# A graph transformer layer on one core: tiles of 125 columns, the values' projection behind the sums, and a different opening

## The chip, the core and the metric

The kernel runs on one core of one Trainium2 chip. The metric is device time in microseconds (us) of one execution, as the median of several runs. A profile is one execution recorded by the hardware. Its engines are TensorE (PE, with its weight loads as PEld), VectorE (DVE), ScalarE (ACT), GpSimd (POOL) and SyncE (SP, which here only issues transfers).

## The reference

The layer takes 3125 nodes of 256 features, 53125 weighted edges sorted by their destination, and the weights of three blocks. All arrays are float32.

```
xn  = layernorm(x)
gnn = segment_sum(edge_weight[:, None] * xn[src], dst) @ W.T + b
q, k, v = xn @ Wq, xn @ Wk, xn @ Wv                # 8 heads of 32
Q, K = elu(q) + 1, elu(k) + 1
KV  = sum over nodes of K^T v, for each head       # 32 x 32 for each of the 8 heads
Z   = 1 / (Q . sum over nodes of K + 1e-6)
msg = layernorm((Q @ KV * Z) @ Wm) * g1 + b1
mix = xn + layernorm(relu([xn, msg] @ W1) @ W2) * g2 + b2
x   = x + gnn + mix
x   = x + ffn(layernorm(x))                        # 16 experts, each node takes the best two
```

What bears on the change is the sum over nodes: `KV = K^T (xn Wv)` is the same as `(K^T xn) Wv`, and the blocks of the heads can be cut out at the end.

## The kernel before

**Tiles.** The 3125 nodes lie in 25 tiles (`NT`) of `V` = 125 nodes. Before the change a tile takes 128 (`P`) rows or columns in most places, of which the last three are padding. Floating point matrices are float32; a float32 matmul is recorded as two MATMUL instructions, a transpose as one.

**The opening.** SP loads the first five tiles of `x` in two transfers (`LOADS`), ACT's queue loads `dst_0` and three weights side by side into `wcat` (L167). PE multiplies ones to keep busy (`busy`, L239), then counts heads of edge lists (L243). DVE takes the mean and variance of the tiles (`stats`, L103 and L104) and their inverse deviations by a chain of thirteen small instructions (`rsqrt`, L91 to L98), one chain for each entry of `BATCHES`: two tiles, three, seven, thirteen. `AHEAD` says at which tile the moments of later tiles are taken. The loads of tiles 5 to 14 wait for the moments of the first batch.

**The projection.** A loop over the tiles runs three things, shifted against each other. In PE's order they stand as T(t+1), P(t), S(t-1):

- `normed(t)`: DVE makes `xn` (L416), PE transposes it in two halves (L428, called T below), ACT copies it to `xnT`.
- `projected(t)`: PE makes messages and keys together, 512 columns wide, in one bank (L437), and values, 256 columns wide, in another (L439); the two are called P. ACT takes exp and relu of the keys, and copies the messages to `y` and the values, with a column of ones behind each half, to `v_sb` (L447). DVE joins the keys (L445). SP stores `y` to DRAM.
- `summed(t)`: PE adds keys times values to `pkv` (L461, 129 columns wide, called S).

Between these DVE, POOL and PE prepare the edge lists in pieces (`windows`, handed out at the tiles that `LISTS` names): the first edge of each group of five nodes, 128 edges gathered behind it, and from them `keys` and `wgts`. Their last steps are three groups of transposes on PE (L309), which stand by T(16), and five conversions on POOL (L317 and L319).

From tile 18 on (`HOT`) each tile also issues two adjacencies. In `adjacency` DVE builds one-hot rows (L335) and weighted ones (L340, L350), PE multiplies twelve pairs of them (L355), ACT copies the result and SP stores it. There are 157 of them; most run in the next stage.

**Behind the sums.** `ksum` and `kv_bd` are the sums of keys and the heads' blocks of `pkv` (L526, L528). PE transposes `kv_bd` (L533) and multiplies it by `Wm` (L538) to give `kvw`. The queries of the first group of tiles (`asked`) are made at tiles 22 and 23 (L477), and are divided by their sums here (L489, four RECIPROCALs of L494).

**The mixer, messages and experts.** Seven groups of four or three tiles go through `mixer` (L641 to L682), where the matmuls of W1 and Wq run over 512 or 384 columns of nodes (L662, L477). Adjacencies and messages (L625) are dealt out between its steps. Then come the last messages (L738) with the gates, and the experts (L1001, L1027).

**Order.** The program is written in one order. The framework places each engine's instructions ahead of time, in that order where their operands are expected to be ready, and later ones ahead where not. Each engine then runs its own list in order.

**PSUM.** There are eight banks: two for adjacencies, two called `big`, three called `tok` and one for `pkv`.

Of the kernel before, what the change touches and what calls it, by code (L numbers as in the profile page):

```python
# [17 lines left out]
N = 3125  # L18
# [35 lines left out]
BATCHES = ((0, 2), (2, 5), (5, 12), (12, 25))  # L54

LISTS = {1: 1, 6: 1, 7: 2, 8: 2, 14: 1, 15: 1, 16: 1}
AHEAD = {1: (2, 5), 2: (5, 9), 3: (9, 12), 4: (12, 15), 6: (15, 17), 9: (17, 21), 10: (21, 25)}
# [5 lines left out]
def tile_gps_layer(ctx: ExitStack, tc: tile.TileContext, a: dict, out: bass.AP):  # L63
# [7 lines left out]
    y_d = dram.tile([NT * P, C], F32, name="y_d")  # L71
# [12 lines left out]
    def rsqrt(var, n, with_last=False):  # L84

        v = small.tile([P, 13], F32, name="rs_v")[:, :n]
        hv = small.tile([P, 13], F32, name="rs_h")[:, :n]
        bits = small.tile([P, 13], I32, name="rs_b")[:, :n]
        y = small.tile([P, 13], F32, name="rs_y")[:, :n]
        s = small.tile([P, 13], F32, name="rs_s")[:, :n]  # L90
# [10 lines left out]
    def stats(mv, src):  # L101
        st = small.tile([P, 6], F32, name="bn_st")
        nc.vector.bn_stats(st, src)  # L103
        return nc.vector.bn_aggr(mv, st)  # L104
# [58 lines left out]
    wcat = w_mix.tile([128, 2, 3 * C], F32, name="wcat")  # L163
    load_x(nc.sync, *LOADS[0])
    nc.scalar.dma_start(dst_0, a["dst"].rearrange("(p j) -> p j", p=V)[:, 0:1])
    for i, name in enumerate(("gnn_WT", "Wk", "Wv")):
        nc.scalar.dma_start(wcat[:, :, i * C : (i + 1) * C], a[name].rearrange("(k p) o -> p k o", p=128))  # L167
    load_x(nc.sync, *LOADS[1])
    wq = w_mix.tile([128, 2, C], F32, name="wq")
    wm = w_mix.tile([128, 2, C], F32, name="wm")  # L170
    w1 = w_mix.tile([128, 4, F], F32, name="w1")
    w2 = w_mix.tile([128, 4, C], F32, name="w2")

    def load_later(t):
# [3 lines left out]
        if t in (11, 13, 15, 17):  # L178
            w, name = ((wm, "Wm"), (wq, "Wq"), (w1, "W1"), (w2, "W2"))[(t - 11) // 2]
            nc.sync.dma_start(w, a[name].rearrange("(k p) o -> p k o", p=128))  # L180
# [16 lines left out]
    xnT = w_mix.tile([128, 2, NT * P], F32, name="xnT")  # L197
# [11 lines left out]
    kv_bd = w_mix.tile([128, 2, 128], F32, name="kv_bd")  # L209
# [9 lines left out]
    def bank_a(of=4 * P):  # L219
        return adj_ps.tile([128, 512], F32, name="pa")[:, :of].rearrange("p (i e) -> p i e", e=of // 4)  # L220

# [7 lines left out]
    def windows():  # L229
# [11 lines left out]
        busy(16)  # L241
# [86 lines left out]
    def adjacency(part, ai, t, n, to):  # L328

        one = hot.tile([128, 2, 2, P, 2], BF16, name="one", bufs=4)  # L330
        wone = hot.tile([128, 2, 3, P, 2], BF16, name="wone")
        if t + 1 < NT:
# [6 lines left out]
            shape = [128, 2, 3, P, 2]  # L339
            nc.vector.tensor_tensor(wone, one[:, :, 1:2, :, :].to_broadcast(shape),  # L340
                                    w[:, :, :, None, :].to_broadcast(shape), op=ALU.mult)
        else:
            for j in range(min(n, 2)):
# [5 lines left out]
                shape = [128, b, 3, P]  # L349
                nc.vector.tensor_tensor(wone[:, :b, :, :, j], one[:, :b, 1:2, :, j].to_broadcast(shape),  # L350
# [941 lines left out]
```

## Time and profile before

| What | Value |
|---|---|
| median of 3 runs | 1037.57 us (1037.27 to 1039.04) |
| the profiled execution | 1038.03 us, of which the span is 1036.2 us |
| PE, share of the span busy | 97% |
| DVE | 63% |
| ACT, POOL | 25%, 21% |
| mean granted PE clock | 0.995 |
| opening and projection | 0 to 111 us |
| mixer with adjacencies and most messages | 121 to 590 us |
| last messages with gates | 591 to 707 us |
| experts | 707 to 1036 us |

The share of a busy engine is taken over its records. PE's records end where a pipeline's model puts the end, so the pace of PE is read from the starts of its instructions: four records of L437 last 1.88 us by their record, while the next line starts 1.72 us later.

### The profile page before, as it was taken

What the parts mean: (1) busy time and instruction counts of PE and PEld (TensorE: products, weight loads), DVE (VectorE), ACT (ScalarE), POOL (GpSimd) and SP (SyncE); (2) the same over time, 40 slices, a digit from 0 to 9 for tenths busy, and PEclk for the clock granted to TensorE, in tenths of its full rate; (3) what the DMA queues carried; (4) which work ended last, traced back from release to release, by engine and by line L of the source; (5) the groups of instructions that cost most, each with busy time, mean ns of one, the idle gap of its engine ahead of it and who ended that gap; (6) DMA issues with size and microseconds to landing.
All of it is one profiled execution on the core that took longest, in us unless ns stands there. A gap on an engine that the chain in (4) does not pass through costs nothing.

```text
span 1036.2 us, 16279 instructions
## 1 busy us (share of the span) xinstructions
PE 1007.1 (97%) x6006; PEld 809.3 (78%) x6006; DVE 655.3 (63%) x1750; ACT 263.9 (25%) x577; POOL 216.1 (21%) x200
## 2 busy tenths in 40 slices
PE   7999999999999999999999999999999999999995
PEld 5667666686786887887877888887888888888884
DVE  8968699889787897956598148786932222222221
ACT  3666424323323233222141000103111111111110
POOL 3420100023100000000000001014445444545442
PEclk9999999999999999999999999999999999999998
DMA  6444104343344344553354455565757757667662
GB/s 214 95 131 145 53 31 167 128 140 136 122 137 138 133 162 133 175 181 143 140 182 155 159 167 166 183 194 179 209 155 226 240 170 234 199 202 225 206 189 26
DMA packets 70374, 165.09 MB, mean 159 GB/s; under 512 B 11091, under 2 KB 29934, under 8 KB 66314
## 3 DMA queue, kind: packets, MB, share of 16 engines
q1 hardware_dynamic: 53816, 138.10, 38.9%
q0 software_dynamic: 15520, 25.04, 10.7%
q8 instruction: 50, 0.82, 0.3%
q10 hardware_dynamic: 946, 0.79, 0.2%
q14 instruction: 42, 0.34, 0.1%
HBM read 105.85 MB, written 58.00 MB: 158 GB/s over the span
## 4 chain that ended last, share of the span: by engine, by line
PE 71%; DVE 10%; issue 1%; POOL 0%; ACT 0%; POOLq 0%; DVEq 0%; ACTq 0%
PE ph L1001 18%; PE pb L625 13%; PE po L1027 10%; PE po L738 8%; PE pa L355 6%; PE big L662 6%; PE tok L673 3%; DVE wone L340 2%; PE ptr L987 1%; PE pa L625 1%; PE big L477 1%; DVE one L335 1%; PE ph L799 1%; DVE wone L350 1%; PE big L489 1%
## 5 line engine op out<-in xcount | busy, mean ns | idle before, releaser
L1001 PE MATMUL ph<-xTb,wt 128*128 128x256 f32 (+2 forms) x992 | 204.5, 355 | 0.8 <-issue 0.8
L1001 PEld LDWEIGHTS ph<-xTb,wt 128*128 128x128 f32 x992 | 171.5, 190 | 24.9 <-ACT xTb L990 4.5
L625 PE MATMUL pb<-y_early,nbr 128*128 128x256 f32 x736 | 170.7, 382 | 0.4 <-DVE x_all L627 0.4
L340 DVE TENSOR_TENSOR wone<-one,wgts 128x1536 bf16<-128x1536 bf16 x150 | 140.6, 949 | 27.0 <-PE pa L355 26.8
L625 PEld LDWEIGHTS pb<-y_early,nbr 128*128 128x128 f32 x736 | 135.4, 190 | 17.2 <-DVE x_all L627 1.0
L355 PEld LDWEIGHTS <-one 128*128 128x128 bf16 x1875 | 117.3, 97 | 39.1 <-issue 19.1
L358 ACT COPY adj<-pa 128x512 f32<-128x512 f32 (+1 forms) x157 | 91.8, 586 | 194.2 <-PE pa L355 156.4
L355 PE MATMUL pa<-wone,one 128*128 128x128 bf16 x1875 | 130.3, 218 | 2.3 <-DVE wone L340 0.9
L1008 DVE TENSOR_TENSOR hid<-hid,ph 128x512 f32<-128x512 f32 (+2 forms) x62 | 38.3, 618 | 145.7 <-PE ph L1001 135.4
L1027 PE MATMUL po<-wt,hid 128*128 128x256 f32 (+1 forms) x456 | 115.2, 385 | 0.8 <-DVE yb L1030 0.7
L738 PE MATMUL po<-y_late,nbr 128*128 128x256 f32 x450 | 102.3, 381 | 0.5 <-DVE x_all L627 0.5
L335 DVE TENSOR_TENSOR one<-iota,keys 128x1024 bf16<-128x1024 bf16 x150 | 100.8, 692 | 0.7 <-POOL wgts L317 0.7
L1031 POOL DMA_INDIRECT out<-yb,to_l x45 | 70.9, 1576 | 114.4 <-DVE yb L1030 63.4
L1027 PEld LDWEIGHTS po<-wt,hid 128*128 128x128 f32 (+1 forms) x456 | 79.1, 184 | 17.6 <-DVE yb L1030 5.5
L738 PEld LDWEIGHTS po<-y_late,nbr 128*128 128x128 f32 x450 | 83.4, 190 | 11.2 <-DVE x_all L627 0.9
L1007 ACT ACTIVATE hid<-ph 128x512 f32<-128x512 f32 (+2 forms) x62 | 33.6, 542 | 208.4 <-PE ph L1001 204.4
L1030 DVE TENSOR_SCALAR yb<-po,sh 128x256 f32<-128x256 f32 (+1 forms) x57 | 27.5, 482 | 57.3 <-PE po L1027 54.9
L751 POOL IOTA rev<- 125x16 f32 x1 | 0.2, 156 | 296.5 <-PE pb L625 296.5
L700 POOL TENSOR_TENSOR x_all<-x_all,cb 128x256 f32<-128x256 f32 x25 | 25.7, 1050 | 148.2 <-DVE x_all L627 140.5
L627 DVE TENSOR_TENSOR x_all<-x_all,pb 128x512 f32<-128x512 f32 (+1 forms) x37 | 24.3, 655 | 41.8 <-PE pb L625 41.8
L662 PE MATMUL big<-xnT,w 128*128 128x512 f32 (+1 forms) x112 | 49.8, 556 | 0.0
L437 PE MATMUL big<-wcat,xnT 128*128 128x512 f32 x100 | 49.0, 612 | 0.0
(285 smaller groups left out, 1202.5 us busy)
## 6 DMA issues: line engine op xcount, KB each, us to landing
wt<-in_w SPq DMA_DIRECT2D x28, 1536.0 KB
adj_d<-adj SPq DMA_DIRECT2D x156, 256.0 KB
nbr<-adj_d SPq DMA_DIRECT2D x25, 576.0 KB
nbr<-adj_d SPq DMA_DIRECT2D x50, 256.0 KB
nbr<-adj_d SPq DMA_DIRECT2D x25, 512.0 KB
wt<-in_w POOLq DMA_DIRECT2D x3, 1536.0 KB
out<-x_all SPq DMA_DIRECT2D x25, 125.0 KB
x_all<-in_x SPq DMA_DIRECT2D x4, 640.0 KB
```

What stands on the lines that cost most here:

```text
L335: nc.vector.tensor_tensor(one.rearrange("p b h e j -> p (b h) e j"), iota_2[:, None, :, :].to_broadcast(shape), ql.rearrange("p b h j -> p ...
L340: nc.vector.tensor_tensor(wone, one[:, :, 1:2, :, :].to_broadcast(shape), w[:, :, :, None, :].to_broadcast(shape), op=ALU.mult)
L355: nc.tensor.matmul(pa[:, j, :], lhsT=one[:, j // 2, 0, :, j % 2], rhs=wone[:, j // 2, i, :, j % 2], start=(i == 0), stop=(i == 2))
L358: copied = nc.scalar.copy(rows[:, :n, :], pa[:, :n, :])
L437: nc.tensor.matmul(pyk, lhsT=xnT[:, k, cols], rhs=wcat[:, k, : 2 * C], start=(k == 0), stop=(k == 1))
L625: nc.tensor.matmul(pb[:, i, :], lhsT=rows[:, k - t0, :], rhs=y_of(k), start=(k == t0 and i == 0), stop=(k == t1 - 1), skip_group_check=True)
L662: nc.tensor.matmul(ph[:, :w], lhsT=w1[:, k, j * 128 : (j + 1) * 128], rhs=rhs, start=(k == 0), stop=(k == 3))
L738: last = nc.tensor.matmul(pg, lhsT=rows[:, k - t0, :], rhs=y_of(k), start=(k == t0), stop=(k == t1 - 1))
L1001: last = nc.tensor.matmul(p[:, m, :w], lhsT=self.wt[:, i, k * F + at : k * F + at + 128], rhs=self.xT[:, k, :w], start=(k == 0), stop=(k = ...
L1008: self.units = nc.vector.tensor_tensor(hid, hid, pre[1], op=ALU.mult)
L1027: last = nc.tensor.matmul(po[:n_r, r, :], lhsT=self.hid[:, k, r * LANES : r * LANES + n_r], rhs=self.wt[:, 2, k * C : (k + 1) * C], start= ...
L1031: made.append(nc.gpsimd.indirect_dma_start(out=out[:, :], out_offset=bass.IndirectOffsetOnAxis(ap=at, axis=0), in_=yb[:n_r, r, :], in_offs ...
```

## The change

**Columns.** Tiles take 125 rows and columns instead of 128: in `xnT`, the transposes, the projections, `y_d`, the adjacencies' weighted rows `wone` and PE's products with them, the queries, the mixer and the messages. Adjacency rows in SBUF keep 128 columns; three buffers (`adj_ring`) have their last three columns set to zero once, by POOL.

**Values.** `Wv` leaves `wcat` and is loaded at tile 9. The projection has no L439 and ACT no copy of values. `xn` gets a column of ones (a ring of six buffers, set by POOL), and the sums run over `xn`: 257 columns wide, each half of the keys in a bank of its own. Behind the sums ACT scales them, PE turns them in four transposes, ACT copies, PE multiplies by `Wv` (eight records of 128 columns) and DVE cuts out the heads' blocks straight into `kvT`; the two old transposes and one copy go.

**PSUM.** `pkv` takes two banks. `tok` has two; when `pkv` is done, one of its banks serves every third `tok`.

**Opening.** The first batch has five tiles, with one chain. The two weights of `wcat` are loaded on SP's queue, behind the first five tiles of `x`. PE keeps busy with 24 products of ones instead of 16.

```diff
-BATCHES = ((0, 2), (2, 5), (5, 12), (12, 25))
+BATCHES = ((0, 5), (5, 12), (12, 25))
-AHEAD = {1: (2, 5), 2: (5, 9), 3: (9, 12), 4: (12, 15), 6: (15, 17), 9: (17, 21), 10: (21, 25)}
+AHEAD = {2: (5, 9), 3: (9, 12), 4: (12, 15), 6: (15, 17), 9: (17, 21), 10: (21, 25)}
...
-    y_d = dram.tile([NT * P, C], F32, name="y_d")
+    y_d = dram.tile([N, C], F32, name="y_d")
...
-    for i, name in enumerate(("gnn_WT", "Wk", "Wv")):
-        nc.scalar.dma_start(wcat[:, :, i * C : (i + 1) * C], a[name].rearrange("(k p) o -> p k o", p=128))
     load_x(nc.sync, *LOADS[1])
+    for i, name in enumerate(("gnn_WT", "Wk")):
+        nc.sync.dma_start(wcat[:, :, i * C : (i + 1) * C], a[name].rearrange("(k p) o -> p k o", p=128))
...
+    def tok(shape):
+        taken_tok.append(0)
+        if spare_ps and len(taken_tok) % 3 == 0:
+            return spare_ps[0].tile(shape, F32, name="tok_3")
+        return a_ps.tile(shape, F32, name="tok")
...
-        busy(16)
+        busy(24)
...
-        wone = hot.tile([128, 2, 3, P, 2], BF16, name="wone")
+        wone = hot.tile([128, 2, 3, V, 2], BF16, name="wone")
...
-                nc.tensor.matmul(pa[:, j, :], lhsT=one[:, j // 2, 0, :, j % 2], rhs=wone[:, j // 2, i, :, j % 2],
+                nc.tensor.matmul(pa[:, j, :V], lhsT=one[:, j // 2, 0, :, j % 2], rhs=wone[:, j // 2, i, :, j % 2],
                                  start=(i == 0), stop=(i == 2))
...
+    xn_ring = [work.tile([P, C + 1], F32, name=f"xn{i}", bufs=1) for i in range(6)]
+    for xn in xn_ring:
+        nc.gpsimd.memset(xn[:, C:], 1.0)
...
-        pv = a_ps.tile([P, C], F32, name="tok", bufs=3)
...
-        for k in range(2):
-            last = nc.tensor.matmul(pv, lhsT=xnT[:, k, cols], rhs=wcat[:, k, 2 * C :], start=(k == 0), stop=(k == 1))
...
-        v_copy = nc.scalar.activation(v_sb[:, :, :128], pv.rearrange("p (c v) -> p c v", c=2), AF.Copy, scale=1.0 / N)
...
-            nc.tensor.matmul(pkv[:, c, :], lhsT=k_sb[:V, c * 128 : (c + 1) * 128], rhs=v_sb[:V, c, :],
-                             start=(t == 0 and c == 0), stop=(t == NT - 1), skip_group_check=True)
+            nc.tensor.matmul(pkv[:, c, : C + 1], lhsT=k_sb[:V, c * 128 : (c + 1) * 128], rhs=xn[:V, :],
+                             start=(t == 0), stop=(t == NT - 1))
...
-    nc.vector.tensor_tensor(kv_bd, same_head[:, None, :].to_broadcast(shape), pkv[:, :, :128], op=ALU.mult)
+    k_by = work.tile([128, 2, C], F32, name="k_by", bufs=1)
+    nc.scalar.activation(k_by, pkv[:, :, :C], AF.Copy, scale=1.0 / N)
+    turned_k = a_ps.tile([128, 512], F32, name="big")
+    for c in range(2):
+        for k in range(2):
+            nc.tensor.transpose(turned_k[:, (2 * k + c) * 128 : (2 * k + c + 1) * 128],
+                                k_by[:, c, k * 128 : (k + 1) * 128], ident)
+    by_k = work.tile([128, 2, 2, 128], F32, name="by_k", bufs=1)
+    nc.scalar.copy(by_k.rearrange("p k c n -> p (k c n)"), turned_k)
+    pvk = tok([128, 2, 128])
+    for c in range(2):
+        for k in range(2):
+            nc.tensor.matmul(pvk[:, c, :], lhsT=wv[:, k, c * 128 : (c + 1) * 128], rhs=by_k[:, k, c, :],
+                             start=(k == 0), stop=(k == 1))
+    kvT = work.tile([128, 2, 128], F32, name="msgT", bufs=1)
+    nc.vector.tensor_tensor(kvT, same_head[:, None, :].to_broadcast(shape), pvk, op=ALU.mult)
```

## The prediction

> **What bounds the kernel now.** I read the page's busy shares first, then busy time by stretch, then the timeline of PE, DVE and POOL up to 125 us, then the groups by line.
>
> ```profile
> PE 1007.1 (97%) x6006; PEld 809.3 (78%) x6006; DVE 655.3 (63%) x1750; ACT 263.9 (25%) x577; POOL 216.1 (21%) x200
> ...
> 14.00:16.00 2.00, 1.47 (x4) 0.81 (x5) 2.00 (x11) 0.37 (x1) 1.52 (x2) 0.78 0.82 303
> 16.00:18.00 2.00, 2.00 (x4) 0.84 (x3) 2.00 (x10) 0.00 (x0) 1.56 (x2) 0.50 0.45 137
> 26.00:52.00 26.00, 26.00 (x115) 17.52 (x114) 23.70 (x81) 15.97 (x49) 11.29 (x13) 1.00 0.46 95
> ```
>
> PE is busy throughout, and its clock (the number before the last two) is whole except at 14 to 19 us. DVE is close behind: 23.70 of 26 us in the projection.
>
> ```profile
> 9.11 1.99 PE L437 MATMUL big<-wcat,xnT 128*128 128x512 f32 x4
> 14.53 0.41 PE L428 MATMUL tok<-ident,xn 128*128 128x128 f32 x2 [2.57 <-DVE less L391]
> 14.77 3.27 PE L437 MATMUL big<-wcat,xnT 128*128 128x512 f32 x4
> 19.72 1.88 PE L437 MATMUL big<-wcat,xnT 128*128 128x512 f32 x4
> ...
> 35.97 1.88 PE L437 MATMUL big<-wcat,xnT 128*128 128x512 f32 x4
> 37.69 1.03 PE L439 MATMUL tok<-wcat,xnT 128*128 128x256 f32 x4
> 38.55 0.61 PE L461 MATMUL pkv<-v_sb,k_sb 125*128 125x129 f32 x4
> 39.00 0.39 PE L428 MATMUL tok<-ident,xn 128*128 128x128 f32 x2
> 39.22 1.88 PE L437 MATMUL big<-wcat,xnT 128*128 128x512 f32 x4
> ```
>
> The opening: P(0) at 9.11, then PE stands 2.57 us for T(2), whose `xn` waits for the second chain of deviations; P(1) then runs at half clock, and P(2) starts at 19.72. From there a tile takes 3.25 us with no gap: 1.72 for L437, 0.86 for L439, 0.45 for L461, 0.22 for the transposes, start to start.
>
> ```profile
> 54.67 0.73 DVE L416 TENSOR_SCALAR xn<-x_all,mv,rs_y 128x256 f32<-128x256 f32 x2
> 61.75 0.70 PE L309 MATMUL pa<-ident,key 125*128 125x125 f32 x5
> 71.15 0.83 POOL L317 CAST wgts<-turned 128x650 bf16<-128x650 f32 x1
> 74.24 1.72 PE L355 MATMUL pa<-wone,one 128*128 128x128 bf16 x24 [0.43 <-DVE wone L340]
> ...
> 111.10 0.42 DVE L526 TENSOR_TENSOR ksum<-same_head,pkv 128x256 f32<-128x256 f32 x1 [0.94 <-PE pkv L461]
> 113.15 3.37 DVE L494 RECIPROCAL eq<-eq 128x256 f32<-128x256 f32 x2 [1.30 <-ACT eq L493]
> 121.81 3.90 PE L641 MATMUL tok<-kvw,qT 128*128 128x256 f32 x16 [0.95 <-DVEq L559]
> ...
> L340 DVE TENSOR_TENSOR wone<-one,wgts 128x1536 bf16<-128x1536 bf16 x150 | 140.6, 949 | 27.0 <-PE pa L355 26.8
> ```
>
> These are the rivals of PE: the edge preparation that leaves xn(16) to 54.67, the conversions on POOL that end at 72 and hold the first adjacency, and the chain of reciprocals behind the sums.
>
> **The change part by part.**
>
> *Opening.* The first statistics start at 4.30, when DVE has `heads`. Two tiles took until 5.30 (the chain's first step); three more at 0.39 each bring it to 6.47. The chain takes as long for five as for two (5.30 to xn(0) at 7.74 is 2.44), so xn(0) comes at 8.91, T(0) at 9.38, P(0) at 10.28. `busy` grows by 16 records of 0.107 us, to about 8.7, in front of the heads' product: DVE wants that product at about 9.8, so it costs nothing, and PE stands idle under 1 us where it stood 2.57. T(2) then waits for no chain; behind xn(1) come about 2 us of L248 to L253, so xn(2) is there at about 11.8, P(1) at 12.4, and with S(0) and T(3) P(2) starts at 15.2, all at whole clock. That is 4.5 us earlier. The next chain must also keep up: moments of seven tiles (2.7), a chain (2.5), three `xn` and three L445 (2.0), factors and three more moments (1.6) from 11.7 put xn(5) at 20.5; T(5) wants it at 20.8.
>
> On the queues: the weights leave ACT's, where nothing waited behind them, for SP's. SP issues them (0.4 us each) while it stands waiting for the first moments anyway. 640 KB of `x` and 512 KB of weights at 350 GB/s (340 to 370 in busy time by stretch, 2.5 to 6 us) have landed by 6 us, before P(0). The loads of tiles 5 to 14 are issued at 6.5 instead of 6.1 and land by 12; moments(5, 9) come at 12. Nothing is charged; without that cover it is under 1 us.
>
> *Values.* L439 leaves with 25 x 0.86 = 21.5 us. L461 goes from 129 to 257 columns, at the 0.84 ns per column of the 256-wide row: 0.86 instead of 0.45, 25 x 0.42 = 10.5 us back. A tile then takes 2.81 us on PE. `Wv` is one more SP issue at tile 9, in a queue with nothing due. ACT loses 25 copies of 0.39 us, which were beside PE. Six columns of ones on POOL fall into its 9.49 us of idling before the first gather. `tok` loses a bank, but a tile takes one instead of two: nothing. The ring of six frees xn(t) after S(t-6), about 8.7 us before T(t) instead of 13: cover for DVE, and at xn(16) DVE is later than that on its own.
>
> *Who is late next.* P(15) would be at 15.2 + 13 x 2.81 = 51.7. DVE: from xn(5) to xn(16) it took 22.23 to 54.67, of which 1.7 idle; from 20.5 that gives 51.2. Both meet; I put the key's L309 at 51.9 instead of 61.75. From there the path goes over PE, ACT, POOL and DVE to the first L355 (61.75 to 74.24, 12.5; 0.2 less with narrower P between), so that comes at 64.2. PE alone needs 12.5 - 0.43 - three times 0.44 = 10.8, so it waits about 1.5 us. From it to the end of the sums (74.24 to 111.06): seven P less 6.0, eight S more 3.4, 14 adjacencies 0.2, L477 0.1: 33.9. The sums end at 98.1, 12.9 earlier.
>
> *Behind the sums.* PE gains 4 - 2 transposes (0.2) and 8 records of 128 columns (0.9); but PE had spare time here, as L641 waits for the reciprocals (113.15 to 120.9). The new DVE product takes the place of `kv_bd` (0.41). Nothing lost if the queries' L489 and reciprocals go first; if they all stand behind the new chain, ACT 0.59, PE 0.7, ACT 0.59, PE 1.1, DVE 0.4 make 3.4 us more. I take 1.0, since `ksum` is ready before the scaled sums.
>
> *Columns elsewhere.* L662: 128 records of 512 lose 12 columns (10 ns), 96 of 384 lose 9 (7.6 ns): 2.0 us. L477 and L489 likewise: 0.6. L355: 1700 records behind the sums, 57.5 ns apart, lose 1.3 ns if the width sets their pace, 2.1 us; nothing if the weights do. No row has a bf16 product 125 wide; the float32 transposes of 125 columns (L309) stand 106 ns apart, those of 128 (L428) 110, so I take two thirds, 1.4. The matmuls 256 wide (L625, L738, L673) don't change, nor do their weights: L461 with 125 rows loads in 191 ns like L437's 190. DVE loses 19 ns for each `wone`. Of 4.0 us, some falls into gaps where PE waits for DVE: 3.4.
>
> *A rule against it.* `y_d` is now written from 125 partitions. The Trainium skill, "DMA: Bandwidth & Descriptors", section "Why a DMA increments its semaphore by 16 and not by 1", says that a transfer is split over the largest number up to 16 that divides its slowest dimension: 5 rings for 125, where 128 had 16. At 350 GB/s over 16 rings, 125 KB then takes 1.2 us (an estimate from that page) instead of 0.4. The trace has stores from 125 partitions (`out`, L742) and an SP issue of 289 ns for them against 320 for `y_d`'s; of their landing it shows nothing. By the row the sum has 0; by the rule five rings get 1.2 us in every 2.81, on which tiles 15 to 24 of `x` queue, wanted over 10 us after issue: also 0, at most 1 us. I take 0.
>
> *Sum.* 12.9 - 1.0 + 3.4 = 15.3. Against the profiled execution's 1038.03 (span 1036.2 and 1.8 around it) that is 1022.7; the median lies 0.46 below it, so 1022.3. The stages after 590 us have the same instructions and move as a block.
>
> **Rivals.**
>
> *Preparation becomes the bound.* The instructions of DVE and POOL for the edges keep more of their place than I gave: gathers land no earlier, or their pieces stand worse in DVE's list. If the first L355 gains only the opening's 4.5 us (69.7), the sums end 7.4 earlier, and the sum is 7.4 - 1.0 + 2.5 = 8.9: 1028.7. For it speaks DVE's 23.70 of 26 us; against it that DVE stood idle 7 us between 26 and 63.
>
> *Slower: `wone` loses its rate.* L335 makes 1024 elements in 692 ns, L340 1536 in 949: 0.5 ns each[...]. Rows of 250 bf16 values start 500 bytes apart, not 512. Should DVE fall to one per cycle, each L340 costs 0.77 us more, 103 us over the 134 behind the sums, where DVE is already 86% busy: 40 to 60 us remain after its idle time, 1072. It decides from about 0.2 us per `wone`. Against it: 500 is a whole number of four-byte pairs, and the output is without gaps.
>
> *The gain isn't there.* If L641 is held by the end of the new chain and the mixer's steps fall differently, 12.9 could be eaten: 1036. PE's unbroken queue from 171 to 530 us speaks against it.
>
> **How the numbers follow.** Measurement of this kernel tells about 0.2% (2 us) from no change. Main case 0.68, 1022.3, own range 1016 to 1029; it gets faster if POOL's 1.5 us is filled and L355 gains fully. Preparation 0.20, 1028.7, from 1025 to 1034. No gain 0.04. Slower 0.08. Faster is 0.68 + 0.20 = 0.88, a little of which lies within 0.2%. The range 1014 to 1031 leaves out the slow case, the empty one and the end of the second.
>
> **What would show it.** P(2) near 15.2 with no half clock before 20 us; P to P 2.81 us; no L439 and L461 at 0.86 for four; the key's L309 at 52, the first L355 near 64 with a wait of about 1.5 us on `wone`; `ksum` near 98; L340 at 930 ns; L355 56.5 ns apart; L641 at about 110. It is wrong if P(3) to P(15) show waits for `xn`, if L340 exceeds 1 us, or if L641 comes over 13 us after the sums.

## The result, and the profile after

The changed kernel takes 1040.79 us (median of seven runs, 1039.08 to 1042.27) where the kernel before takes 1037.70 in the same job: ratio 1.0028, 95% interval 1.0019 to 1.0037. It is slower by some 3 us. The forecast was 1022.3, 15 us faster. The profiled execution of the changed kernel took 1039.08, its span is 1037.2; the two profiled executions differ by 1.0 us only, so the tables below tell where time is won and lost, and the medians how much in all.

First the spans of the stages, each from the start of one instruction to the start of the next. The last column is a version with four amendments that is told below; it shows what the change is worth when nothing gives it back.

| Stage | Before | Changed | Forecast of the difference | Amended |
|---|---|---|---|---|
| start to `ksum` (end of the sums) | 111.10 | 108.23 | -12.9 | 100.05 |
| `ksum` to the mixer's first product | 10.71 | 10.67 | +1.0, here or in the next row | 10.65 |
| from there to group 0's first W2 product | 24.09 | 28.58 | | 24.04 |
| from there to the last messages | 445.11 | 444.82 | -3.4 | 442.55 |
| last messages and gates | 117.49 | 117.38 | 0 | 116.46 |
| experts to the end of the span | 327.7 | 327.5 | 0 | 327.6 |

The changed kernel gains 2.9 us up to the sums, loses 4.5 behind them, and the narrower columns give 0.3 in the long stage after them. These are the three places to look at. Lines have moved by about ten: the transposes are L439, P(t) is L447, S(t) is L466, the joined keys L453, the key's transposes L319, the adjacency products L365.

The page's busy shares and busy time by stretch (length, then busy time of PE, PEld, DVE, ACT, POOL with the number of instructions, clock, DMA share, GB/s):

```profile
PE 1002.6 (97%) x5932; PEld 800.2 (77%) x5932; DVE 648.2 (62%) x1732; ACT 255.5 (25%) x553; POOL 217.5 (21%) x209
...
14.00:16.00 2.00, 0.15 (x1) 0.00 (x0) 2.00 (x16) 1.42 (x4) 0.75 (x1) 1.00 0.76 182
16.00:18.00 2.00, 0.87 (x4) 0.82 (x5) 1.83 (x13) 0.00 (x0) 1.69 (x2) 1.00 0.95 310
26.00:52.00 26.00, 24.36 (x81) 14.39 (x82) 21.52 (x83) 12.23 (x37) 10.96 (x13) 0.93 0.47 105
```

PE loses 4.5 us of busy time, and the time doesn't follow. From 14 to 17 us PE stands while DVE is busy without a gap. From 26 to 52 us, where PE never stood before, it is idle for 1.6 us and its clock is 0.93.

PE's timeline (start, duration, line, out<-in, and in brackets the idle time ahead and its releaser):

```profile
10.23 1.98 PE L447 MATMUL big<-wcat,xnT 128*125 128x512 f32 x4
12.27 1.88 PE L447 MATMUL big<-wcat,xnT 128*125 128x512 f32 x4
17.13 1.10 PE L466 MATMUL pkv<-xn,k_sb 125*128 125x257 f32 x4 [2.98 <-DVE rs_s L98]
18.28 3.48 PE L447 MATMUL big<-wcat,xnT 128*125 128x512 f32 x4
...
27.64 1.10 PE L466 MATMUL pkv<-xn,k_sb 125*128 125x257 f32 x4 [2.98 <-DVE mv L105]
28.91 3.46 PE L447 MATMUL big<-wcat,xnT 128*125 128x512 f32 x4
33.28 1.88 PE L447 MATMUL big<-wcat,xnT 128*125 128x512 f32 x4
35.00 1.03 PE L466 MATMUL pkv<-xn,k_sb 125*128 125x257 f32 x4
...
36.09 1.88 PE L447 MATMUL big<-wcat,xnT 128*125 128x512 f32 x4
```

P(0) and P(1) come as forecast, at 10.23 and 12.27. Then S(0) stands 2.98 us, P(2) runs at half clock, and the same happens again at S(2) and P(4). P(5) starts at 33.28, later than the 29.5 of before. From there a tile takes 2.80 us (33.28 to 36.09), with S(t) at 0.87: these parts of the sum hold. The releasers named in brackets are small steps that ended last by chance; what S(0) reads is `k_sb(0)`, the joined keys of tile 0. DVE's and POOL's timeline show it:

```profile
12.17 0.78 DVE L258 TENSOR_TENSOR cmp_h<-pa,thr 125x625 f32<-125x625 f32 x1
14.76 0.15 DVE L263 CAST row_i<-row_f 125x5 int32<-125x5 f32 x1
15.25 1.41 POOL L267 DMA_INDIRECT rows<-in_dst,row_i  x1 [11.65 <-DVE mv L105]
16.59 0.39 DVE L453 SCALAR_TENSOR_TENSOR k_sb<-ek,k_sb 125x256 f32<-125x256 f32 x1
24.70 0.60 DVE L277 TENSOR_TENSOR cmp_r<-rows,thr 125x425 bf16<-125x425 int32 x1 [4.89 <-DMA rows<-in_dst,row_i]
27.08 0.41 DVE L453 SCALAR_TENSOR_TENSOR k_sb<-ek,k_sb 125x256 f32<-125x256 f32 x1
```

ACT has the operands of `k_sb(0)` ready at 12.9 (its second activation runs from 12.53 for 0.38 us). DVE joins them at 16.59, since its list has the moments of tiles 5 to 11, parts of their chain and the heads' comparison ahead. The comparison is interleaved with those moments, so `row_i` comes at 14.76 and the first gather starts at 15.25 (12.88 before). Its rows land at 24.7: DVE stands 4.89 us for them, and `k_sb(2)` is queued behind.

The kernel before had the same late keys, without harm:

```profile
12.88 1.41 POOL L257 DMA_INDIRECT rows<-in_dst,row_i  x1 [9.49 <-DVE rs_s L97]
15.57 0.38 DVE L445 SCALAR_TENSOR_TENSOR k_sb<-ek,k_sb 128x256 f32<-128x256 f32 x1
19.05 0.61 PE L461 MATMUL pkv<-v_sb,k_sb 125*128 125x129 f32 x4
```

There ACT had the operands of `k_sb(0)` ready at 11.8 and DVE joined them 3.8 us later, as in the changed kernel (12.9 and 16.59). But PE stood for T(2) first and came to S(0) only at 19.05. The change took that wait away, and so the next one behind it came to light.

Rows answering to the rest of those shown of before, among them the one-hot rows and the adjacency products by group (count, then busy time in us and mean ns of one):

```profile
61.08 0.70 PE L319 MATMUL pa<-ident,key 125*128 125x125 f32 x5
73.50 1.67 PE L365 MATMUL pa<-wone,one 128*128 128x125 bf16 x23 [1.76 <-DVE wone L350]
...
108.23 0.42 DVE L534 TENSOR_TENSOR ksum<-same_head,pkv 128x256 f32<-128x256 f32 x1 [1.23 <-PE pkv L466]
118.90 0.65 PE L661 MATMUL tok<-kvw,qT 128*125 128x256 f32 x2
...
L350 DVE TENSOR_TENSOR wone<-one,wgts 128x1500 bf16<-128x1500 bf16 x150 | 138.0, 932 | 28.9 <-PE pa L365 28.6
L365 PE MATMUL pa<-wone,one 128*128 128x125 bf16 x1875 | 134.8, 222 | 2.8 <-DVE wone L350 2.6
```

The key's transposes come only 0.7 us earlier than before (61.75), and the way from there to the first adjacency is as long as it was (12.42, before 12.49). DVE keeps its rate at 932 ns. But L365, three columns narrower, has grown from 218 ns (130.3 us busy) to 222 (134.8).

Behind the sums, DVE's timeline in the changed kernel, and below the dots the first and last line of the same chain before:

```profile
125.97 0.17 DVE L92 TENSOR_SCALAR rs_v<-mv_m 125x4 f32<-125x4 f32 x1
...
127.64 0.16 DVE L99 SCALAR_TENSOR_TENSOR rs_y<-rs_s,rs_y 125x4 f32<-125x4 f32 x1
127.72 1.71 DVE L499 RECIPROCAL eq<-eq 128x250 f32<-128x250 f32 x1
129.35 0.10 DVE L97 TENSOR_TENSOR rs_s<-rs_y 125x4 f32<-125x4 f32 x1
129.36 1.70 DVE L499 RECIPROCAL eq<-eq 128x250 f32<-128x250 f32 x1
130.98 0.10 DVE L98 TENSOR_TENSOR rs_s<-rs_s,rs_h 125x4 f32<-125x4 f32 x1
132.00 1.05 DVE L669 TENSOR_SCALAR mw<-mw,mv_m,rs_y 125x256 f32<-125x256 f32 x3
...
126.43 0.17 DVE L91 TENSOR_SCALAR rs_v<-mv_m 128x4 f32<-128x4 f32 x1
129.37 1.05 DVE L649 TENSOR_SCALAR mw<-mw,mv_m,rs_y 128x256 f32<-128x256 f32 x3
```

Two reciprocals of the next queries stand between three steps of group 0's deviation chain that take 0.1 to 0.2 us each. From the chain's first step (125.97) to the first normalised message it is 6.0 us; before it was 2.9 (126.43 to 129.37), with the reciprocals behind.

### The profile page after: what moved, and what is told of

It is laid out like the page before. It is cut to its first block, busy times and chain, and to the rows that moved or that the text cites. A ratio compares the mean times of both kernels' runs of the same rounds, so it can differ in the third digit from the quotient of the medians.

```text
span 1037.2 us, 16080 instructions
## 1 busy us (share of the span) xinstructions
PE 1002.6 (97%) x5932; PEld 800.2 (77%) x5932; DVE 648.2 (62%) x1732; ACT 255.5 (25%) x553; POOL 217.5 (21%) x209
## 4 chain that ended last, share of the span: by engine, by line
PE 72%; DVE 9%; issue 1%; POOL 0%; ACT 0%; POOLq 0%; DVEq 0%; ACTq 0%
PE ph L1021 18%; PE pb L645 13%; PE po L1047 10%; PE po L758 8%; PE pa L365 7%; PE big L682 5%; PE tok L693 3%; DVE wone L350 2%; PE ptr L1007 1%; PE pa L645 1%; PE big L482 1%; DVE one L345 1%; PE ph L819 1%; PE big L494 1%; DVE bn_st L104 1%
## 5 line engine op out<-in xcount | busy, mean ns | idle before, releaser
L645 PE MATMUL pb<-y_early,nbr 125*125 125x256 f32 x736 | 170.6, 382 | 0.3 <-DVE x_all L647 0.3
L350 DVE TENSOR_TENSOR wone<-one,wgts 128x1500 bf16<-128x1500 bf16 x150 | 138.0, 932 | 28.9 <-PE pa L365 28.6
L365 PEld LDWEIGHTS <-one 128*128 128x128 bf16 x1875 | 121.6, 98 | 38.8 <-issue 18.7
L645 PEld LDWEIGHTS pb<-y_early,nbr 125*125 125x125 f32 x736 | 133.9, 188 | 18.5 <-DVE x_all L647 0.9
L368 ACT COPY adj<-pa 128x500 f32<-128x500 f32 (+1 forms) x157 | 91.0, 580 | 198.2 <-PE pa L365 181.2
L365 PE MATMUL pa<-wone,one 128*128 128x125 bf16 x1875 | 134.8, 222 | 2.8 <-DVE wone L350 2.6
L758 PE MATMUL po<-y_late,nbr 125*125 125x256 f32 x450 | 102.3, 381 | 0.5 <-DVE x_all L647 0.5
L758 PEld LDWEIGHTS po<-y_late,nbr 125*125 125x125 f32 x450 | 82.4, 188 | 12.1 <-DVE x_all L647 0.9
L647 DVE TENSOR_TENSOR x_all<-x_all,pb 125x512 f32<-125x512 f32 (+1 forms) x37 | 24.3, 657 | 43.5 <-PE pb L645 43.2
L682 PE MATMUL big<-xnT,w 128*128 128x500 f32 (+1 forms) x112 | 49.0, 550 | 1.9 <-ACT qT L486 1.2
L447 PE MATMUL big<-wcat,xnT 128*125 128x512 f32 x100 | 50.8, 631 | 0.0
```

The lines of the kernel that those rows point to most:

```text
L350: nc.vector.tensor_tensor(wone, one[:, :, 1:2, :V, :].to_broadcast(shape), w[:, :, :, None, :].to_broadcast(shape), op=ALU.mult)
L365: nc.tensor.matmul(pa[:, j, :V], lhsT=one[:, j // 2, 0, :, j % 2], rhs=wone[:, j // 2, i, :, j % 2], start=(i == 0), stop=(i == 2))
L368: copied = nc.scalar.copy(rows[:, :n, :V], pa[:, :n, :V])
L447: last = nc.tensor.matmul(pyk, lhsT=xnT[:, k, cols], rhs=wcat[:, k, :], start=(k == 0), stop=(k == 1))
L645: nc.tensor.matmul(pb[:V, i, :], lhsT=rows[:V, k - t0, :V], rhs=y_of(k)[:V], start=(k == t0 and i == 0), stop=(k == t1 - 1), skip_group_ch ...
L682: nc.tensor.matmul(ph[:, :w], lhsT=w1[:, k, j * 128 : (j + 1) * 128], rhs=rhs, start=(k == 0), stop=(k == 3))
```

## Experiments

The theory: the change's gains are there, and the order of DVE's list gives them back, at three points: the first joined keys, the gather's rows, the mixer's chain. Apart from this, L365's rows have a slower start. The rival: DVE and POOL are simply late with the preparation, whatever their order. Runs of different jobs are compared by their ratios to the kernel before, whose median lay between 1036.1 and 1039.3 from job to job; a difference of ratios is turned into us with 1037.7.

**DVE's order in the opening.** Moments and preparation pieces are held behind `row_i` and behind the joined keys of tile t - 3. No computation is changed.

```diff
+    def behind(t):
+        with ExitStack() as those:
+            if len(joined) > t - 3 >= 0:
+                those.enter_context(tc.issue_after(joined[t - 3].ins))
+            if heads_found:
+                those.enter_context(tc.issue_after(heads_found[0].ins))
+            return those.pop_all()
...
-                next(pieces, None)
+                with behind(t):
+                    next(pieces, None)
...
-                moments(*AHEAD[t])
+                with behind(t):
+                    moments(*AHEAD[t])
```

> The changed kernel with three orders on VectorE alone: the moments taken ahead stand behind the count of the list heads and behind the joined keys of three tiles before, and so do the pieces of the edge preparation. No instruction is added or taken away. If the place of the joined keys in VectorE's list is the cause of both 2.98 us waits of the sums and of the two stretches at half clock, both are gone: P(2) at about 15.2 us instead of 18.3, P(5) at about 23.6 to 26 instead of 33.3, the clock whole from 9 us on, and the sums end 6 to 9 us earlier, 1032 to 1035. If the cause is the data (late loads, late gathers), the waits move to other instructions and P(5) stays near 33.

Measured: 1033.89 us, ratio 0.9942 (0.9926 to 0.9959). PE's timeline (P(t) is L461 in this run, S(t) L480):

```profile
11.27 1.98 PE L461 MATMUL big<-wcat,xnT 128*125 128x512 f32 x4
15.84 1.10 PE L480 MATMUL pkv<-xn,k_sb 125*128 125x257 f32 x4 [0.66 <-DVE k_sb L467]
17.00 1.88 PE L461 MATMUL big<-wcat,xnT 128*125 128x512 f32 x4
...
25.40 1.88 PE L461 MATMUL big<-wcat,xnT 128*125 128x512 f32 x4
```

One wait of 0.66 is left, no tile runs at half clock, and P(5) starts at 25.40 instead of 33.28, though P(0) happened to come 1.0 later. The key's transposes start at 56.53, `ksum` at 101.41. Behind the sums nothing has changed (4.5 us more than before, as in the changed kernel). With the same instructions in another order, 8.9 us are back by the ratios (1.0028 less 0.9942, about 1.9 us either way). In the two profiles the sums end 6.8 us earlier (101.41 against 108.23); the other 2 us are within the noise and were not located. The rival, which leaves the order no part, falls.

**Each order alone.** Only `row_i` ahead of the moments:

> The changed kernel with half of the ordering: moments and preparation pieces stand behind the copy of the gather's first rows (so that the comparison with the heads and the rows of the gather come ahead of the moments of tiles 5 to 14), and nothing is said of the joined keys. The gathers start about 2 us earlier than 15.25, so the rows' comparison waits for nothing at 27 us and the second wait of TensorE (2.98 at 27.64, with half clock after it) should go; the first (2.98 at 17.13) should stay, since the first joined keys stand behind the moments still. Theory A (each of the two waits costs its length and about 1.7 us of half clock, some 4 us together): P(2) near 18.3, P(5) near 28, time half way between the changed kernel and the one with both orders, ratio to the kernel before 0.998 to 0.999. Rival B (what counts is only when the gathered rows are there, since the preparation ends later than the projection's tiles need): nearly all of the gain of both orders, ratio 0.994 to 0.996.

Measured: ratio 0.9981 (0.9974 to 0.9989). The first gather starts at 13.20. The waits of S(t) are 1.41, 1.50 and 0.76, P(5) is at 28.2, `ksum` follows the last S(t) at 102.8.

> The changed kernel with the other half of the ordering: moments and preparation pieces of tile t stand behind the joined keys of tile t - 3, and nothing is said of the gather's rows, which stay behind the moments of tiles 5 to 8. The first wait of TensorE (2.98 at 17.13) should shrink below 1 us, P(2) at 16 to 17; the gathers stay near 15 us, so the rows' comparison still waits at about 25 and with it the joined keys behind it: the second wait stays at 2 to 4 us. Theory A: half of the gain, ratio 0.998 to 0.999. Rival B (the gather's rows are what counts): the gain of the first wait is lost in the second and the preparation ends where it did, ratio 1.001 to 1.003.

Measured: ratio 0.9965 (0.9952 to 0.9978). S(0) waits 0.63, P(5) is at 24.4, but then the rows, gathered from 14.74 on, hold DVE 2.77 us and S(4) 1.32 us; P(6) is at 28.8. In both the last S(t) starts near 102.6 (102.81 and 102.39), where both orders together give 100.24 and the changed kernel 107.06. By the ratios the first order gives 4.9 us and the second 6.5, of 8.9 for both. So each alone gives more than half, and the rivals that gave all to one of them fall. Theory A's number is met by the first (0.998 to 0.999) and beaten by the second, and its waits fell otherwise than expected, since the first order shortened the first wait too. In the second run's profile some 1.3 us are lost in another place: after a wait of 1.96 us at the first adjacency PE's clock fell to half, which it didn't do in the run with both orders.

**The opening, apart from the rest.** The changed kernel with the opening of before (batches 0 to 1 and 2 to 4, weights on ACT's queue, 16 products), and the kernel before with the new opening alone:

```diff
-BATCHES = ((0, 5), (5, 12), (12, 25))
+BATCHES = ((0, 2), (2, 5), (5, 12), (12, 25))
...
-        busy(24)
+        busy(16)
```

> The changed kernel with the old opening: batches of two and three tiles, weights on ACT's queue, 16 products of ones. If the opening is what ate the gain of the projection, the sums end as far before 111 us as the narrower tiles make them, about 23 tiles of 0.44 us, so near 101 to 103 us instead of 108, and the time is 1034 to 1037. If the opening is not at fault (the loads, the wider sums or the missing tok bank are), P(5) comes no earlier than the 33.3 us of the changed kernel and the time stays at 1040.

> The kernel before with the new opening alone: one batch of five, weights on SP's queue behind x, 24 products of ones. If the opening's placement of the joined keys is at fault by itself, this is slower than the kernel before by the two waits and the half clock: P(5) at 33 to 36 us where it was 29.5, time 1041 to 1046. If the opening only fails together with the narrower projection, it gains what was forecast for it, P(2) at 16 instead of 19.7, time 1033 to 1035.

Measured: the old opening in the changed kernel gives 1042.51, ratio 1.0035 (1.0021 to 1.0049), where a good deal less was expected. P(5) comes at 27.7, 5.6 us earlier than in the changed kernel, but S(t) then stands 3.17 us at 49.74, and the key's transposes start at 60.71. The joined keys that it stands for are queued on DVE behind the conversion of the gathered window (L296), ahead of which DVE stands 4.03 us for a DMA, until 46.31. The wait has moved, not gone. The new opening in the kernel before gives 1043.28, ratio 1.0033 (1.0022 to 1.0045): there, too, S(t) waits for joined keys (0.61 at 16.97, 2.19 at 22.65, then half clock), P(5) comes at 31.9, and the first adjacency at 76.65 instead of 74.24. By itself it is a loss, as the first theory had it.

**The start of L365's rows.** The rows of `wone` again 512 bytes apart, with 125 columns computed and used:

```diff
-        wone = hot.tile([128, 2, 3, V, 2], BF16, name="wone")
+        wone = hot.tile([128, 2, 3, P, 2], BF16, name="wone")[:, :, :, :V, :]
```

> The changed kernel with the weighted rows kept 125 wide but laid 512 bytes apart instead of 500. The products of the adjacencies stood 60.0 ns apart with the change, 57.5 before. If the start of a row that is no multiple of 64 bytes costs the 2.5 ns, they return to 57.5 or a little under (56.2 at 125 columns), and the kernel gains 1875 x 2.5 to 3.8 ns, 4 to 6 us, of which most shows: 1035 to 1037. If it is the width of 125 itself, or the writes to PSUM, they stay at 60 and the time stays at 1040 to 1041. The two compared operands are two bytes wide with a step of two either way, so VectorE's 932 ns should not move by more than 10.

Measured: 1039.95, ratio 1.0004 (0.9997 to 1.0010), 2.5 us below the changed kernel by the ratios, where 4 to 6 were expected. The group's row:

```profile
L365 PE MATMUL pa<-wone,one 128*128 128x125 bf16 x1875 | 130.1, 218 | 3.5 <-DVE wone L350 2.2 <-ACT adj L368 0.4
```

24 products take 1.36 to 1.38 us again instead of 1.44, and from the W2 products to the last messages it takes 442.6 instead of 444.8 us. (In this execution the second wait of the opening was longer, 4.13 us, so its first stage isn't to be compared.) The narrower width itself moves the pace by less than 0.5 ns; the distance of 500 bytes costs 2.5 ns per product (60.0 against 57.5).

> The changed kernel with the weighted one-hot rows of the adjacency laid out by turns with six distances from row to row: 125, 126, 128, 132, 136 and 144 elements of 4 bytes (500, 504, 512, 528, 544 and 576 bytes), each with its products on a line of its own; 125 columns are used of every row. With 500 bytes throughout a stage of 24 products takes 1.44 us, with 512 bytes 1.37. Theory A (the start of a row against a boundary of 64 bytes sets the pace): 512 and 576 bytes at 57 to 57.5 ns per product, the other four at 60. Theory B (a boundary of 32 bytes): 544 too at 57.5. Theory C (a boundary of 16 bytes): 528 too. Theory D (only rows that start on an odd multiple of 4 bytes pay): all but 500 at 57.5. Of the time nothing is expected but that it lies between 1038 and 1042.

Measured in one kernel with six distances by turns, in the order 500, 504, 512, 528, 544, 576 bytes:

```profile
L369 PE MATMUL pa<-wone,one 128*128 128x125 bf16 x315 | 23.3, 222 | 1.9 <-DVE wone L353 1.8
L372 PE MATMUL pa<-wone,one 128*128 128x125 bf16 x312 | 22.9, 221 | 0.0
L375 PE MATMUL pa<-wone,one 128*128 128x125 bf16 x312 | 22.3, 219 | 0.4 <-DVE wone L353 0.4
L378 PE MATMUL pa<-wone,one 128*128 128x125 bf16 x312 | 22.6, 220 | 0.1
L381 PE MATMUL pa<-wone,one 128*128 128x125 bf16 x312 | 22.3, 219 | 0.6 <-ACT adj L387 0.4
L384 PE MATMUL pa<-wone,one 128*128 128x125 bf16 x312 | 22.3, 219 | 0.3 <-ACT adj L387 0.3
```

The means differ by little; start to start, 12 products (median of about 25 undisturbed stretches each) take 0.72 us at 500 bytes, 0.71 at 504, and 0.69 at each of the other four. Theory C stands, by a single execution with a resolution of 0.01 us in 0.7. Read product by product, the traces say it more sharply. Twelve products read six rows of a tile in turn, and with a distance of 500 bytes only rows 0 and 4 start at a multiple of 16 bytes (0 and 2000, counted from the start of the tile). In the changed kernel the step from a product of these two rows to the next takes 56 to 58 ns, from one of the other four rows 59 to 63 (medians of 150 groups). With 504 bytes, in the run above, rows 0, 2 and 4 take 56 to 58 and rows 1, 3 and 5 take 59 to 62; with 512 all six take 56 to 58. So it is the start of each row that counts: at a multiple of 16 bytes it has the full pace, at other multiples of 4 or 8 it hasn't.

**The reciprocals behind the chain.**

```diff
-            if next(following, "end") != "end":
+            with tc.issue_after(found.ins):
+                more_left = next(following, "end") != "end"
+            if more_left:
```

> The changed kernel with one thing more: in the mixer, the steps of the next query's features are issued behind the last instruction of the deviation chain, so that on VectorE the two reciprocals of the next queries (L499 at 127.72 and 129.36) no longer stand in the middle of group 0's chain (from 125.97 to the first normalised message at 132.00, 6.0 us; 2.9 us in the kernel before). Theory A (the list's order on VectorE lengthens the path behind the sums): the chain is back at 2.9 to 3.2 us, group 0's W2 products start near 144.5 instead of 147.5, everything after is about 3 us earlier, ratio to the kernel before near 1.000 where the changed kernel has 1.0028. Rival B (TensorE fills the longer chain with adjacency products that it would have to do anyway, so nothing is lost there): the chain is shorter, but the last messages start within 0.5 us of 592.3 and the ratio stays at 1.003.

Measured: 1036.82, ratio 1.0009 (1.0000 to 1.0017). DVE's timeline:

```profile
127.48 0.17 DVE L92 TENSOR_SCALAR rs_v<-mv_m 125x4 f32<-125x4 f32 x1
...
130.42 1.05 DVE L669 TENSOR_SCALAR mw<-mw,mv_m,rs_y 125x256 f32<-125x256 f32 x3
```

The chain is back at 2.9 us, and from the mixer's first product to W2 it takes 25.6 us instead of 28.6. Theory A holds: 2.0 us by the ratios, 3.0 in that stage. (In this execution the opening's waits were longer, 2.59 and 3.62, so its first stage isn't to be compared.)

**The first queries on both sides of the new chain.**

```diff
+    next(queries[0])
     k_by = work.tile([128, 2, C], F32, name="k_by", bufs=1)
...
-    for _ in range(2):
-        next(queries[0])
+    next(queries[0])
```

> The changed kernel with one of the two steps of the first queries issued ahead of the kv chain (scaling, turning, values' projection, mask) and the other behind it, instead of both behind it. In the changed kernel the first reciprocal starts 3.05 us after the sum of keys is masked (2.05 us before), and the mixer's first product follows later. Theory A (the values' projection, now behind the sums, stands ahead of the queries' chain on its engines): the first reciprocal is back near 2.05 us after the mask, the mixer starts about 1 us earlier, time about 1 us below the changed kernel (ratio to the kernel before 1.001 to 1.003). Rival B (the mixer waits for kvw, which needs the mask and two more products and copies, and these come later now): the reciprocals are earlier, but the first mixer product is where it was or later, and the time is the same or 0.5 us worse.

Measured: 1038.24, ratio 1.0020 (1.0013 to 1.0028). The first reciprocal is back at 2.03 us behind `ksum`, as theory A has it, and the mixer's first product is where it was (10.67 behind `ksum`), as the rival has it. The gain lies between. In the changed kernel PE's list has only two of the mixer's products first and then one of W1:

```profile
120.74 1.11 PE L682 MATMUL big<-xnT,w 128*128 128x500 f32 x2 [1.20 <-ACT qT L486]
```

It stands 1.20 us until ACT has emptied a bank of `big` that holds queries of the next group (L486); the other 14 of the mixer's products come behind it. In this run the queries of group 0 are ready 10.0 us behind `ksum` instead of 11.5, twelve products stand ahead of W1's, this wait is gone, and the way to W2 takes 27.1 instead of 28.6. By the ratios it is 0.8 us, and the intervals overlap.

**All four together.**

> All that the experiments point to, together: the changed kernel with VectorE's moments and preparation pieces of the opening held behind the joined keys (measured alone: 1033.9), rows of the weighted one-hots 512 bytes apart (measured alone: 0.9 to 2.5 us), the next queries' reciprocals behind the deviation chain, and the first queries' steps on both sides of the kv chain. Theory A (the four losses lie one behind the other on the path): 1033.9 - 2.3 - 3 - 1 = 1027.6, between 1026 and 1030, ratio about 0.989. Rival B (they share their waits, so that the first takes most of it): 1031 to 1034, ratio about 0.994.

Measured: 1023.72, ratio 0.9881 (0.9866 to 0.9896), which is theory A's ratio: it beats both kernels, and by 1.2% the one before. The page and the timelines:

```profile
PE 994.7 (97%) x5932; PEld 795.0 (78%) x5932; DVE 647.6 (63%) x1732; ACT 254.8 (25%) x553; POOL 216.9 (21%) x209
...
26.00:52.00 26.00, 26.00 (x95) 15.70 (x94) 22.20 (x78) 15.56 (x47) 10.33 (x12) 1.00 0.56 140
...
55.45 0.75 PE L319 MATMUL pa<-ident,key 125*128 125x125 f32 x5 [0.32 <-DVE key L307]
100.05 0.42 DVE L548 TENSOR_TENSOR ksum<-same_head,pkv 128x256 f32<-128x256 f32 x1 [1.23 <-PE pkv L480]
```

PE has the same 5932 instructions and is busy 7.9 us less than in the changed kernel: half clock and the slow pace of L365 count as busy there. The parts alone give 8.9, 2.5, 2.0 and 0.8, together 14.2 us; measured together it is 15.2 (1.0028 less 0.9881). The stages of the first table show the same: against the changed kernel 8.2 us are won up to the sums, 4.5 from the mixer to W2 and 2.3 from there to the last messages. The losses lie one behind the other on the path.

**Two variants of it.** The old opening in the amended version, and the late preparation pieces one tile earlier:

> The version with all four amendments (1023.7), but with the opening of the kernel before: chains of deviations for tiles 0 to 1 and 2 to 4, the weights on ScalarE's queue ahead of tiles 2 to 4 of x, 16 warming products. Theory A (the new opening is worth what it takes from P(2), once VectorE's list does not give it back): P(2) near 19.5 instead of 16.0, everything up to the sums' end 3 to 4 us later, ratio 0.991 to 0.992. Rival B (the preparation's VectorE list sets when the adjacency starts, in either opening): first adjacency within 1 us of 67.9, ratio 0.988 to 0.989, so that the opening gives nothing.

Measured: ratio 0.9905 (0.9891 to 0.9919), 2.5 us above the amended version by the ratios. P(2) is at 16.42, only 0.45 us later than in the amended version: with DVE's list in order, P(1) follows P(0) at once and doesn't wait for the second chain. P(5) is at 25.62 (24.38 in the amended version), the first adjacency at 69.16 (67.94), `ksum` at 102.54 (100.05). Of these 2.5 us the opening shows 1.2; the other 1.3 are the clock, here against the amended version below it:

```profile
69.16 2.34 PE L365 MATMUL pa<-wone,one 128*128 128x125 bf16 x24 [1.96 <-DVE wone L350]
...
67.94 1.70 PE L365 MATMUL pa<-wone,one 128*128 128x125 bf16 x24 [1.98 <-DVE wone L350]
```

After waits of the same length it fell to half in one execution (0.81 on average from 66 to 75 us) and not in the other. Whether this belongs to the opening was not tested. Neither theory's number was met, A's was missed narrowly, and its P(2) near 19.5 was wrong.

```diff
-            if len(joined) > t - 3 >= 0:
-                those.enter_context(tc.issue_after(joined[t - 3].ins))
+            back = 4 if t >= 14 else 3
+            if len(joined) > t - back >= 0:
+                those.enter_context(tc.issue_after(joined[t - back].ins))
```

> The version with all four amendments (1023.7), and the preparation pieces of tiles 14 to 16 one tile earlier in VectorE's list (behind the joined keys of tile t - 4 instead of t - 3), where VectorE stands idle 1.19 and 2.05 us at 39.8 and 41.8. Theory A (the preparation on VectorE sets the first adjacency, at which TensorE waits 1.98 us): the conversion of the window starts near 42 instead of 44.1, the wait at the first adjacency falls to 0 to 0.7 us, time 1.3 to 2 us less, ratio 0.986 to 0.987. Rival B (the window's rows land no earlier than 44, or the joined keys now stand behind a piece and TensorE waits for them instead): ratio 0.988 or above.

Measured: ratio 0.9889 (0.9875 to 0.9904), no gain. DVE's timeline:

```profile
42.78 0.60 DVE L296 CAST src_f<-win 125x640 f32<-125x640 int32 x1 [1.24 <-DMA g<-in_g]
```

The window's conversion starts 1.4 us earlier and then stands for a DMA. The profile names a load behind the window's gather on the same queue; what the conversion reads is the gathered window. So here it is the gather that bounds the preparation. The key's transposes come at 54.44 and the first adjacency at 66.91, each about 1 us earlier, but `ksum` comes at 101.21, 1.2 us later. PE's timeline shows the loss ahead of these transposes, as the rival had it: joined keys now stand behind a piece.

```profile
46.29 1.13 PE L481 MATMUL pkv<-xn,k_sb 125*128 125x257 f32 x4 [0.30 <-DVE k_sb L468]
```

The same happens at 49.52 and 52.79 (0.17 and 0.20), and from P to P it is 3.37 and 3.24 us there instead of 2.80. The first adjacency comes earlier in time, but with one tile less done before it: seven P(t) stand behind it instead of six.

## Why the prediction was wrong

**Opening.** The failed step is "with S(0) and T(3) P(2) starts at 15.2, all at whole clock". P(0), the five moments, one chain and the 24 products came as worked out (P(0) 10.23 against 10.28). For that S(0) had to start near 14.1; it started at 17.13, after a wait of 2.98 us. The working counted DVE's joined keys in its sum, but asked only whether `xn` keeps up, not where `k_sb(0)` stands in the list. In the source, moments and pieces are hung on the `xn` of a tile. With one chain for five tiles the first five `xn` come at once, and what hangs on them came ahead of the first joined keys. The keys had been as late before (15.57), hidden behind the wait that the change took away. P(2) was at 18.28; in the amended version it is at 16.0, the rest being a wait of 0.65. The working also had L248 to L253, the comparison that ends in `row_i`, right behind `xn(1)`; moments came among its steps, the gather started at 15.25, and DVE stood 4.89 us for its rows. That second wait decided: in the run with split queries the clock did not fall after the first wait, P(3) came at 21.1 instead of 22.8, and S(2) still started no earlier (27.85).

**Who is late next.** "I put the key's L309 at 51.9" was the next failed step: 61.08, and 56.5 and 55.45 with the order mended. The working carried on DVE's instructions from xn(5), and the gather's rows and windows were not in it; one variant shows DVE waiting for the window at 42.8. Why 3.5 us are left in the amended version is not settled beyond that. The steps behind it held within 2 us: 12.3 us to the first adjacency (12.42 and 12.49), a wait of about 1.5 (1.76 and 1.98), then 33.9 to the end of the sums (34.7 and 32.1).

**Behind the sums.** Bounded at 0 to 3.4 and taken as 1.0, it was 4.5. The place was wrong too: "L641 over 13 us after the sums" was to be the sign, and the mixer starts 10.67 us after them, as before. The loss comes later, from reciprocals in the middle of the mixer's chain (about 3 us) and from the later queries, by which a product of W1 came ahead of the mixer's own and stood for a bank (about 1.5).

**Columns.** The term of L355 was taken as -1.4; 60.0 ns against 57.5 on 1700 products is +4.2 us, of which 2.3 reach the end of the mixed stage (444.82 against 442.55). In that stage the narrower columns gave 0.3 instead of 3.4; with rows 512 bytes apart they gave 2.6 (445.11 to 442.55), so the sum's 2.6 for the products other than L355 was about right. The forecast considered only that width or weights set the pace, not where a row starts.

**Right.** The tile at 2.80, S(t) at 0.87, L350 at 932 ns (the slower rival falls), nothing lost by the weights' queue as far as P(0) shows, and no sign that the stores of `y_d` from 125 partitions hold anything: tiles keep their 2.80 us through them. Also the amended kernel: 0.9881 of 1037.7 is 1025.4, 3 us from the forecast. The sum was about right for a list in which nothing is late, and the kernel doesn't have that list. None of the three signs of being wrong showed: PE stood for joined keys, which none of them named. Of the rivals, the preparation's (0.20) named a part of the mechanism, gathers no earlier and pieces that stand worse in DVE's list, but left 8.9 us of gain. "The gain isn't there" was given 0.04; its 1036 comes nearest to the measured time, by other causes than it named in the main.

## What to carry to other kernels

When a change makes operands come earlier or all at once, read the list of every in-order engine anew: what hangs on those operands moves ahead of what the critical engine waits for, and the busy sum of the engine doesn't show it. Ask for each short instruction on the path (here joined keys of 0.4 us and chain steps of 0.2) what stands ahead of it. Taking away a wait shows the next one behind it, so ask too what was late before without harm. And narrowing a tile is two changes: its width, and the place where each of its rows starts; keep the distance between rows when only the width should change.

## What was not expected of the hardware

A bf16 product of 125 columns whose moving rows lie 500 or 504 bytes apart took 60.0 or 59.2 ns from start to start on average; at 512, 528, 544 and 576 bytes it took about 57.5. Within a group only the products whose row starts off a multiple of 16 bytes are slow, 59 to 63 ns against 56 to 58. VectorE wrote such rows at an unchanged 932 to 933 ns.

The clock of TensorE fell to half after standing 1.97 us (P(2) took 3.41 in the run with 512-byte rows), 2.19 and 2.98, but not after 2.97 in the run with split queries (P(2) took 1.88), nor after 1.3 to 1.5. At the first adjacency it fell after 1.96 us in two runs and did not after 1.96 and 1.98 in two others. So the length of a wait alone doesn't decide. In the changed kernel the granted clock is at half for 3.4 us each time, from 18.3 to 21.8 and from 28.7 to 32.1; both stretches begin about 1 us after the wait has ended. The Trainium skill, "TensorE: Matmul & The Clock Gate", section "Part 1: The HAM clock gate (the "warmup" mystery)", says that the clock is set by the activity in a free-running window; that would fit, though its 3.4 us of idle time are longer than these waits. In the changed kernel each fall made one P(t) 1.6 us longer (3.48 and 3.46 against 1.88).
